# Latent attention and the start of a six-layer pipeline: keys and values from a folded weight, another split of small copies over two queues, and three pieces of work moved to other places

## The chip, the cores and the metric

The kernel runs on one core of one Trainium2 chip. A core has a matrix engine (PE, TensorE; PEld is its weight load), VectorE (DVE), ScalarE (ACT), GpSimd (POOL), and SyncE (SP), which here only issues DMAs. ScalarE and GpSimd can issue DMAs too. Each engine works through its own instruction list in order, and waits on semaphores for the others.

The metric is the device time of one execution in microseconds (us), lower is better. Times below are in us unless ns is said.

## The reference

Four residual blocks, each on the layer-normed stream, over 16 sequences of 256 tokens of 128 features, all in float32:

```python
x = x + latent_attention(layernorm(x), Wq, bq, Wl, bl, Wk, bk, Wv, bv, Wo, bo)   # 16 heads of 8
x = x + six_layers(layernorm(x), ...)    # 16 heads of 64, window 32, each with a gated MLP of 341
x = x + mamba(layernorm(x), ...)
x = x + two_layers(layernorm(x), ...)    # 8 heads of 64, window 64, each with a gated MLP of 341
```

The first of them is what most of the change touches:

```python
q = (x @ Wq + bq).reshape(B, S, H, Dh)
latent = x @ Wl + bl                       # 32 features
k = (latent @ Wk + bk).reshape(B, S, H, Dh)
v = (latent @ Wv + bv).reshape(B, S, H, Dh)
scores = jnp.einsum('bihd,bjhd->bhij', q, k) * SCALE
attn = jax.nn.softmax(scores, axis=-1)
out = jnp.einsum('bhij,bjhd->bihd', attn, v).reshape(B, S, D)
out = out @ Wo + bo
```

In a layer of the six, the output of attention is multiplied by a matrix Wo of 1024 rows, 64 per head; the value projection Wv has 64 columns per head.

## The kernel before

**Latent attention** (`latent_attention`). The 4096 tokens are cut into 8 tiles t of 512 tokens, that is two sequences. Three generators and four functions deal with a tile:

- `prepare(t)` transposes the tile, norms it (`normed`: a matmul with the centering matrix, squares on ScalarE, a matmul for the mean, rstd on GpSimd at L116, transposes of rstd at L167), makes the 32 latent features (L278, L280), and from them keys (L297) and values (L303); queries come from the normed x (L284). It has eight steps, divided by `yield`. All of them and `finish` use one PSUM bank (`bank`, pool la_m with one buffer).
- `spread`, within `prepare`, copies queries and keys, 16 small DMAs each (8 rows of 512), into padded tiles qa and ka, of which there are three of each. They go to SP and GpSimd in turn (L291).
- `maximum(m)` makes scores with PE (L328) and takes their row maxima with VectorE (L337); `subtract` writes the maxima, transposed, into a spare row of qa (L354, a DMA of ScalarE's queue); `weigh(m)` makes the transposed scores (L366) and exponentials (L376); `apply(m)`, for odd m only, multiplies with the values (L389) and copies the result to os (L398).
- `gather(t)` undoes the padding with 32 small DMAs, 16 to `sums` and 16 to `of` (L412): one row group in four on SP, the rest on GpSimd; of the last tile one half on each.
- `finish(t)` takes the reciprocal of the sums (L418), multiplies (L419), multiplies with Wo (px, L422), adds to x (L423), stores x to HBM (L424) and norms the result into the tile y, which the six layers read.

The loop at L432 runs m from -12 to 130, in an order written out by hand (`manual_schedule`): what is emitted first stands first on each engine. Tile t has the sixteen m from 16t on for `weigh`; `maximum` is 12 ahead. In each m there are the matmuls of `weigh(m)` and `maximum(m+12)` by turns, then either a `subtract` or one step of the generators in the list `steps`, then `apply(m-2)`. `prepare(t)` joins the list at m = 16(t-2), `finish(t)` at m = 16(t+1)+10, where its first step is emitted at once, ahead of the matmuls; `gather(t)` is emitted as a whole at m = 16(t+1)+1. What is emitted outside of such a stretch may be put earlier on an engine by the scheduler.

**The six layers** (`Pipeline` with PLAN32). A block is 128 tokens, 32 blocks a layer. In iteration i of `run`, the list PLAN32 names the steps and how many blocks each lags; block i is projected to q and k (L782) in iteration i. I call iteration i "block i" below. Norms of pairs of blocks come from a Newton iteration on GpSimd (`pair_newton`, L852 to L858), the output of a pair of blocks is multiplied with wvo, the product of Wv and Wo per head (L1086), five blocks later. wvo of a later layer is made two heads at a time beside `turn_y` in the blocks of the layer before (`coming`, `products`, `keep_y`). wvo of the first layer, and the offsets of its MLP (`offsets`, `add_offsets`), are made at i = 3, all at once, in `rest_of_ready` (L672). At i = 6 the `finish` of the last tile of latent attention, returned by it as `rest`, is run through at once. PSUM has four double banks here; the list after PLAN32 says which step uses which: pq, scores and the tiles pb and pm of `rest_of_ready` share one (o); yt, tk, tq, tp and u0 share another (s); `rest` uses q.

`load(0)` issues the first layer's weights on SP: wqkv in two halves, the scales sc, wo, wv, w1, w2. It comes after latent attention, since the weights take its place in memory. `tables` makes the rotation table from sc with VectorE (L690, L692).

Of the kernel before, what the change touches and what calls it, by code (L numbers as in the profile page):

```python
# [29 lines left out]
P = 128  # L30
# [158 lines left out]
def latent_attention(ctx: ExitStack, k: Stack, w, x_in, last, later):  # L189
# [9 lines left out]

    nc = k.nc
    H, D, LAT = 16, 8, 32
    SCALE = D**-0.5
# [7 lines left out]


    wq = wp.tile([P, P], F32, name="wq")
    wk = wp.tile([LAT, P], F32, name="wk")
    wl = wp.tile([P, LAT], F32, name="wl")
    wv = wp.tile([LAT, P], F32, name="wv")
    wo = last.tile([P, P], F32, name="wo")
    bq, bk, bo = (p.tile([P, 1], F32, name=n) for n, p in (("bq", wp), ("bk", wp), ("bo", last)))
    bl = wp.tile([LAT, 1], F32, name="bl")  # L220
    bv = wp.tile([P, P], F32, name="bv")
    for t, name in ((wl, "Wl"), (wq, "Wq"), (wk, "Wk"), (wv, "Wv"), (wo, "Wo")):
        nc.scalar.dma_start(t, w[name])
    for t, name in ((bl, "bl"), (bq, "bq"), (bk, "bk"), (bo, "bo")):
        nc.scalar.dma_start(t, w[name].unsqueeze(1))
# [32 lines left out]
    def prepare(t):  # L258

        ps = bank()  # L260
        xt = xs.pop(t)
        for j in range(4):
            nc.tensor.transpose(ps[:, j * P : (j + 1) * P], xt[:, j, :], k.ident)
        if 3 <= t + 2 < NTT:
            fetch(t + 2)
        pool = last if t == NTT - 1 else work
        x = xs[t] = pool.tile([P, TT], F32, tag="x", bufs=1 if t == NTT - 1 else 5, name=k.name("x"))
        nc.scalar.copy(x, ps)
        yield
        for step in k.normed(x, bank):  # L270
            if step is None:
                yield
        cen, ps = step
        xn = work.tile([P, TT], F32, tag="xn", bufs=1, name=k.name("xn"))
        nc.vector.tensor_mul(xn, cen, ps)
        yield
        ps = bank()
        nc.tensor.matmul(ps[0:LAT], wl, xn, start=True, stop=True)  # L278
        lat = work.tile([LAT, TT], F32, tag="lat", bufs=1, name=k.name("lat"))
        nc.scalar.activation(lat, ps[0:LAT], AF.Identity, bias=bl)  # L280
        yield
        q, kk = (work.tile([P, TT], F32, tag=i, bufs=1, name=k.name(i)) for i in "qk")
        ps = bank()
        nc.tensor.matmul(ps, wq, xn, start=True, stop=True)  # L284
        nc.vector.tensor_scalar(q, ps, bq, SCALE, ALU.add, ALU.mult)
        queues = (nc.sync, nc.gpsimd)

        def spread(src, dst):
            for r in range(4):
                for g in range(4):  # L290
                    queues[g % 2].dma_start(dst[32 * r : 32 * r + D, g], src[rows_of(r, g)])  # L291

        nc.sync.dma_start(qa[t % 3][D::32], row[:, 0:1].to_broadcast([4, 4, TT]))
        spread(q, qa[t % 3])
        yield
        ps = bank()
        nc.tensor.matmul(ps, wk, lat, start=True, stop=True)  # L297
        nc.scalar.activation(kk, ps, AF.Identity, bias=bk)
        spread(kk, ka[t % 3])
        yield  # L300
        ps = bank()
        for c in range(4):
            nc.tensor.matmul(ps[:, bass.ts(c, P)], lat[:, bass.ts(c, P)], wv, start=True, stop=True)  # L303
        nc.vector.tensor_add(
            va[t % 3][:, :, :, 0:D],
            ps.rearrange("p (c h d) -> p c h d", c=4, d=D),
            bv.rearrange("p (h d) -> p h d", d=D).unsqueeze(1).to_broadcast([P, 4, H, D]),
        )
        yield

    nms, oss, weights, outs = {}, {}, {}, {}

# [87 lines left out]
    def gather(t):  # L400

        os = oss.pop(t)
        o, sums = (
            (last if t == NTT - 1 else work).tile([P, TT], F32, tag=i, bufs=1, name=k.name(i))
            for i in ("of", "sums")
        )
        for dst, first in ((sums, D), (o, 0)):
            for r in range(4):
                rows = slice(32 * r + first, 32 * r + first + D)
                for g in range(4):  # L410
                    queue = nc.sync if g == 3 or (t == NTT - 1 and g == 2) else nc.gpsimd
                    queue.dma_start(dst[rows_of(r, g)], os[rows, g])  # L412
        outs[t] = o, sums

    def finish(t, bank):

# [8 lines left out]
        yield  # L425
        yield from k.norm_to_y(t, x, bank)

    for _ in prepare(0):
        pass
    AHEAD, steps = 12, []  # L430
    with k.tc.manual_schedule():
        for m in range(-AHEAD, 8 * B + 3):  # L432
            at = m + AHEAD
            if at == 0 or (at % 16 == 12 and at // 16 + 2 < NTT):
                steps.append(prepare(1 if at == 0 else at // 16 + 2))
            if at == 14:
                later()
            if m % 16 == 10 and m > 16:
                steps.append(finish(m // 16 - 1, bank))
                next(steps[-1])  # L440
            four = (
                weigh(m) if 0 <= m < 8 * B else (),
                maximum(at) if at < 8 * B else (),
            )
            for _ in zip_longest(*four):
                pass
            if at % 4 == 1 and 2 <= at <= 8 * B + 1:
                subtract(at - 2)
            else:
                while steps and next(steps[0], True):  # L450
                    steps.pop(0)
            if 2 <= m <= 8 * B + 1:
                apply(m - 2)
            if m % 16 == 1 and m > 16:
                gather(m // 16 - 1)
    return lambda bank: finish(NTT - 1, bank)


# [82 lines left out]
class Pipeline:  # L541
# [124 lines left out]

    def ready(self, l):

        self.tables(l)
        self.rest_of_ready(l)  # L670

    def rest_of_ready(self, l):  # L672
        k, nc, L = self.k, self.nc, self.layers[l]
        pb = k.wide(self.homes["scores"], "pb")[:, 0:6]
        self.offsets(l, pb)
        self.add_offsets(l, pb)
        if self.W == 64:
            return
        for c0 in (0, 4):
            pm = k.wide(self.homes["scores"], "pm").rearrange("p (i c d) -> p i c d", i=2, d=P)  # L680
            for c in range(4):
                self.products(l, c0 + c, pm[:, :, c])
            nc.scalar.copy(
                L.wvo[:, 2 * c0 : 2 * c0 + 8].rearrange("p (c i) d -> p i c d", i=2), pm
            )

    def tables(self, l):

# [40 lines left out]

    def coming(self, n):  # L730

        l, step = divmod(n, NBLK)
        return l + 1, step if l + 1 < self.depth else -1

    @staticmethod
    def beside(yt):

        return yt[:, P : P + 768].rearrange("p (i d) -> p i d", i=2)[:, :, 0:P]

    def run(self, rest=None):  # L740

        last = self.depth * NBLK
        self.work = self.work or self.pool("work", 2)
        if self.W == 64:
            self.ready(0)
        else:
            self.tables(0)
        with self.k.tc.manual_schedule():
            for i in range(last + max(lag for _, lag in self.plan)):
                if i % NBLK == 14 and i // NBLK + 1 < self.depth:  # L750
                    self.load(i // NBLK + 1)
                if i == 3 and self.W == 32:
                    self.rest_of_ready(0)
                if i == 6 and rest:
                    for _ in rest(lambda: self.k.wide(self.homes["norm"], "rest")[:, 0:TT]):
                        pass
                for (name, *args), lag in self.plan:
                    n = i - lag
                    if not 0 <= n < last:
                        continue  # L760
                    if name.startswith("ff_"):
                        if n % 4 == 0:
                            getattr(self, name)(n // 4, *args)
                    elif name.startswith("pair_"):
                        if n % 2 == 0:
                            getattr(self, name)(n, *args)
                    else:
                        getattr(self, name)(n, *args)
# [140 lines left out]
    def turn_y(self, n):  # L909

        L, b, blk = self.at(n)
        t0 = self.W + blk * P
        yt = self.bank(n, "yt")
        self.nc.tensor.transpose(yt[:, 0:P], self.k.y[:, b, t0 : t0 + P], self.k.ident)
        l, step = self.coming(n)
        if step == 17:
            self.tables(l)
        if 18 <= step < 26:
            self.products(l, step - 18, self.beside(yt))
        if step == 26:  # L920
            self.offsets(l, yt[:, P : P + 6])

    def keep_y(self, n):
# [2 lines left out]
        l, step = self.coming(n)  # L926
        if 18 <= step < 26:
            c = 2 * (step - 18)
            self.nc.scalar.copy(self.layers[l].wvo[:, c : c + 2], self.beside(yt))
        if step == 26:  # L930
            self.add_offsets(l, yt[:, P : P + 6])

    def spread(self, n):
# [614 lines left out]
def tile_kernel(ctx: ExitStack, tc: tile.TileContext, a, out):  # L1548
# [8 lines left out]
    with ExitStack() as stack:  # L1557
# [2 lines left out]
        rest = latent_attention(k, every("L0_attn_"), a["L0_attn_x"], last, pipe.setup)  # L1560
        with k.pairs():
            pipe.open()
            pipe.run(rest)
    with ExitStack() as stack:
        pipe = Pipeline(k, stack, part("L1_ffn_"), 8, 64, a["rope64"], 2, PLAN64, out)
        pipe.setup()
# [31 lines left out]
```

## Time and profile before

| | us |
|---|---|
| median of 3 runs (lowest to highest) | 4891.48 (4888.69 to 4897.18) |
| profiled execution, its own time | 4885.07 |
| its span, first to last instruction | 4883.2 |
| mean granted TensorE clock (1 is full) | 0.974 |
| latent attention, first scores to last `apply` | 34 to 420 |
| first load of wqkv issued | 420.5 |
| filling of the six-layer pipeline | 420 to about 600 |

Busy time of the engines within the stretch from 290 to 335 us, one period of latent attention, and the idle time before the operation and what ended it:

| operation | engine | count | mean ns | idle before |
|---|---|---|---|---|
| L328, scores | PE | 136 | 401 | 1.5, for the reductions L337 |
| L366, transposed scores | PE | 136 | 402 | 0.1 |
| L389, values | PE | 128 | 385 | 0 |
| L167, transposes of rstd | PE | 8 | 285 | 2.6, for GpSimd L116 |
| L337, maxima | DVE | 33 | 688 | 13.9, for L328 |
| L418, reciprocal | DVE | 1 | 3345 | 0 |
| L376, exponentials | ACT | 33 | 595 | 10.0 |
| L412, gathers to sums | POOL | 12 | 523 | 1.4 |
| L291, spreads of keys | POOL | 8 | 519 | 0 |

A float32 matmul appears as two records, so the counts of PE are twice those in the code; four matmuls with 32 rows run beside one another, so their records overlap. The issue of a DMA is busy time on GpSimd, but not on SP or ScalarE. A wait is counted for the engine that stands still, and named after what came last.

### The profile page before, as it was taken

Reading aid. Unit: us, or ns where it says so; the run is one execution under the profiler, and the core shown is the slowest. Engines: PE = TensorE matmul, PEld = TensorE weight load, DVE = VectorE, ACT = ScalarE, POOL = GpSimd, SP = SyncE. Lnnn points to the kernel's source line nnn. Section 1 sums busy time; section 2 is a strip of 40 time slices with the busy share of each in tenths; the row PEclk is TensorE's granted clock in tenths of the full one; section 3 lists DMA queues with packets and bytes.
Section 4 is the critical chain, followed back from the end, with each engine's and each line's share of the span. In section 5 each row is a group of like instructions: output and inputs, shape, how many; then the busy total and the mean of one; then the engine's idle time right before and its main releaser. Section 6 shows DMA issues by size and latency. Waiting matters only on the chain.

```text
span 4883.2 us, 121363 instructions
## 1 busy us (share of the span) xinstructions
PE 4587.9 (94%) x50842; PEld 3063.1 (63%) x50842; DVE 3372.6 (69%) x4048; ACT 2743.4 (56%) x3417; POOL 3317.8 (68%) x3643
## 2 busy tenths in 40 slices
PE   8896799999999999999999999999996998899998
PEld 4453566666666666666666666666664665566665
DVE  4663677777777777777777777777772765788774
ACT  3553466566656666566666566665663453565654
POOL 3444677777777777777777777787783454777774
PEclk9997899999999999999999999999998898999999
DMA  1111010000100010001000010000101000111111
GB/s 35 37 29 43 14 39 17 16 16 18 39 16 16 17 39 16 16 17 39 16 16 16 17 39 16 17 17 22 26 23 41 15 12 18 53 47 43 49 56 39
DMA packets 208778, 131.54 MB, mean 27 GB/s; under 512 B 62029, under 2 KB 180153, under 8 KB 208233
## 3 DMA queue, kind: packets, MB, share of 16 engines
q1 hardware_dynamic: 196456, 118.12, 9.7%
q0 software_dynamic: 9984, 5.14, 0.6%
q8 instruction: 403, 6.60, 0.6%
q14 instruction: 143, 1.16, 0.1%
q10 hardware_dynamic: 1792, 0.51, 0.1%
HBM read 29.65 MB, written 8.39 MB: 8 GB/s over the span
## 4 chain that ended last, share of the span: by engine, by line
PE 69%; DVE 14%; POOL 7%; issue 5%; ACT 4%; SPq 0%; DMA 0%; DVEq 0%; ACTq 0%; POOLq 0%
PE py L1086 13%; PE pq L782 7%; PE hid L1143 6%; PE u L1060 6%; PE scores L973 5%; PE pk L782 5%; PE tq L872 4%; PE tp L1019 3%; DVE n L839 3%; PE fy L1177 3%; PE tk L872 2%; DVE rotq L807 2%; POOL rstd L116 1%; PE scores L955 1%; DVE t2q L819 1%
## 5 line engine op out<-in xcount | busy, mean ns | idle before, releaser
L1086 PE MATMUL py<-oT,wvo 128*128 128x256 f32 x3072 | 679.1, 379 | 1.2 <-ACT oT L1073 1.2
L1013 POOL TENSOR_TENSOR pr<-pr,rs 128x1024 f32<-128x1024 f32 x256 | 489.8, 1913 | 273.5 <-DVE rs L1008 241.4
L843 POOL TENSOR_TENSOR rotq<-rotq,t2q 128x1024 f32<-128x1024 f32 x256 | 605.0, 2363 | 37.0 <-DMA w<-in_L_ffn_W 22.2
L1086 PEld LDWEIGHTS py<-oT,wvo 128*128 128x128 f32 x3072 | 577.1, 190 | 75.1 <-ACT oT L1073 1.6
L1073 ACT COPY oT<-u 128x1024 f32<-128x1024 f32 x384 | 377.5, 1014 | 316.3 <-PE u L1060 307.6
L782 PE MATMUL pq<-wqkv,y 128*128 128x512 f32 x1024 | 495.6, 607 | 15.3 <-DVE t2q L819 5.4
L863 POOL TENSOR_TENSOR rotq<-rotq,rn 128x1024 f32<-128x1024 f32 x256 | 488.8, 1909 | 11.2
L807 DVE TENSOR_TENSOR rotq<-pq,tab 128x1024 f32<-128x1024 f32 x256 | 313.4, 1224 | 235.9 <-ACT sqq L793 150.5
L101 DVE TENSOR_TENSOR y<-y,py 64x256 f32<-64x256 f32 x256 | 107.2, 419 | 524.7 <-PE py L1086 523.0
L889 ACT COPY qT<-tq 128x1024 f32<-128x1024 f32 (+1 forms) x256 | 230.7, 901 | 410.9 <-PE tq L872 410.9
L843 POOL TENSOR_TENSOR rotk<-rotk,t2k 128x1024 f32<-128x1024 f32 x192 | 454.0, 2364 | 0.0
L1004 DVE TENSOR_REDUCE rs<-pr 128x16 f32<-128x1024 f32 (+1 forms) x256 | 312.3, 1220 | 157.7 <-ACT pr L997 152.9
L973 PEld LDWEIGHTS scores<-kT,qT 64*32 64x32 f32 (+1 forms) x26624 | 320.7, 108 | 157.9 <-issue 97.2
L793 ACT ACTIVATE sqq<-pq 128x1024 f32<-128x1024 f32 x256 | 261.8, 1023 | 263.1 <-PE pq L782 250.7
L1060 PE MATMUL u<-prT,vc 64*128 64x256 f32 x3072 | 405.5, 395 | 1.9
L973 PE MATMUL scores<-kT,qT 64*32 64x64 f32 (+2 forms) x26624 | 398.8, 225 | 3.0 <-issue 1.4
L782 PE MATMUL pk<-wqkv,y 128*128 128x512 f32 x768 | 393.3, 602 | 6.8 <-DMA wqkv<-in_L_ffn_Wqkv 6.8
L1143 PE MATMUL hid<-fxn,w 128*128 128x512 f32 (+1 forms) x768 | 388.9, 618 | 5.4 <-DVE ga L1165 2.7
L852 POOL TENSOR_SCALAR rn<-n 128x64 int32<-128x64 int32 (+1 forms) x128 | 30.3, 236 | 530.6 <-DVE n L839 530.6
L863 POOL TENSOR_TENSOR rotk<-rotk,rn 128x1024 f32<-128x1024 f32 x192 | 365.4, 1903 | 0.1
L997 ACT ACTIVATE pr<-pr 128x1024 f32<-128x1024 f32 x256 | 270.6, 1057 | 135.9 <-DVE pr L989 122.2
L984 DVE TENSOR_REDUCE nm<-scores 128x16 f32<-128x1024 f32 (+1 forms) x256 | 312.1, 1219 | 22.0 <-PE scores L973 20.6
(265 smaller groups left out, 9835.2 us busy)
## 6 DMA issues: line engine op xcount, KB each, us to landing
vc<-vt SPq DMA_DIRECT2D x1152, 32.0 KB
vc<-vt SPq DMA_DIRECT2D x64, 256.0 KB
vc<-vt SPq DMA_DIRECT2D x96, 128.0 KB
vc<-vt SPq DMA_DIRECT2D x576, 16.0 KB
xd<-x SPq DMA_DIRECT2D x24, 256.0 KB
wqkv<-in_L_ffn_Wqkv SPq DMA_DIRECT2D x12, 512.0 KB
x<-xd SPq DMA_DIRECT2D x24, 256.0 KB
wo<-in_L_ffn_Wo SPq DMA_DIRECT2D x6, 512.0 KB
```

The lines of the kernel that those rows point to most:

```text
L782: self.nc.tensor.matmul(pq[:, 512 * int(half) : 512 * int(half) + 512], self.k.y[:, b, c0 : c0 + P], L.wqkv[:, col : col + 512], start=Tru ...
L807: self.nc.vector.tensor_mul(rot.rearrange("p (w h) e -> p w h e", w=ways), self.get(n, "p" + group).rearrange("p (w h e) -> p w h e", w=wa ...
L843: self.nc.gpsimd.tensor_add(rot, rot, self.done(n, "t2" + group))
L863: self.nc.gpsimd.tensor_mul(rot, rot, rn.unsqueeze(2).to_broadcast(list(rot.shape)))
L973: self.nc.tensor.matmul(sc[ch * W : (ch + 1) * W, par, c, first : self.KS], qT[rows, c, ch * W : (ch + 1) * W], kT[rows, c, t0 - W + first ...
L984: self.nc.vector.tensor_reduce(nm, self.get(n, "scores"), AX.X, ALU.max, negate=True)
L1004: self.nc.vector.tensor_reduce(rs, self.by_head(n), AX.X, ALU.add)
L1013: self.nc.gpsimd.tensor_mul(pr, pr, rs)
L1060: self.nc.tensor.matmul(pu[:, par, :, j, :], self.vc[n % 3][rows, ch, :], prT[rows, :, ch * W : (ch + 1) * W], start=True, stop=True,)
L1073: self.nc.scalar.copy(self.get(n - blk, "oT")[:, :, q0 : q0 + 64].rearrange("p (c i) q -> p i c q", i=2), self.done(n, "u" + half).rearran ...
L1086: self.nc.tensor.matmul(py, w[:, c, :], oT[:, c, :], start=(c == 0), stop=(c == last))
L1143: self.nc.tensor.matmul(pg[0:n, at : at + TT], L.w1[:, col : col + n], self.get(t, "fxn"), start=True, stop=True,)
```

## The change

- The host gives the transposed Wl as well (WlT). A new function `fold`, called after the second step of `prepare(0)`, multiplies Wl with Wk and with Wv, and bl with them for the biases. Keys and values come straight from the normed x with these 128x128 weights; the step with the latent features is gone, so `prepare` has seven steps.
- Spreads go to SP alone from tile 2 on; tiles 0 and 1 keep the turns of SP and GpSimd.
- Gathers go to GpSimd alone, but for the last tile, half of which stays on SP. `gather` is a generator of eight steps with four DMAs each, one step in each m from 16(t+1)+1 on. What is left of it after the loop is emitted behind the loop, outside of the order written out by hand.
- `finish(t)` joins at m = 16(t+1)+11, one later, and behind the step of that m.
- First layer: `rest_of_ready` is gone. `products` come beside `turn_y` in blocks 1 to 4, four heads each, and the offsets in block 6; `keep_y` copies them.
- The `finish` of the last tile is run one step a block from block 3 on.

```diff
+    wk0, wv0, wlT = (wp.tile([LAT, P], F32, name=n) for n in ("wk0", "wv0", "wlT"))
+    wk, wv = (wp.tile([P, P], F32, name=n) for n in ("wk", "wv"))
...
-        ps = bank()
-        nc.tensor.matmul(ps[0:LAT], wl, xn, start=True, stop=True)
-        lat = work.tile([LAT, TT], F32, tag="lat", bufs=1, name=k.name("lat"))
-        nc.scalar.activation(lat, ps[0:LAT], AF.Identity, bias=bl)
-        yield
...
-        queues = (nc.sync, nc.gpsimd)
+        queues = (nc.sync, nc.gpsimd if t < 2 else nc.sync)
...
-        nc.tensor.matmul(ps, wk, lat, start=True, stop=True)
+        nc.tensor.matmul(ps, wk, xn, start=True, stop=True)
...
-            nc.tensor.matmul(ps[:, bass.ts(c, P)], lat[:, bass.ts(c, P)], wv, start=True, stop=True)
+            nc.tensor.matmul(ps[:, bass.ts(c, P)], xn[:, bass.ts(c, P)], wv, start=True, stop=True)
...
+    def fold():
+        for dst, of, bias, lhsT, rhs in (
+            (wk, wk0, None, None, None),
+            (wv, wv0, None, None, None),
+            (bk, None, bk, wk0, bl),
+            (bv, None, bv, bl.to_broadcast([LAT, P]), wv0),
+        ):
+            ps = bank()[:, 0 : dst.shape[1]]
+            if of is not None:
+                nc.tensor.matmul(ps, wlT, of, start=True, stop=True)
+                nc.scalar.copy(dst, ps)
+            else:
+                nc.tensor.matmul(ps, lhsT, rhs, start=True, stop=True)
+                nc.vector.tensor_add(dst, bias, ps)
...
-                    queue = nc.sync if g == 3 or (t == NTT - 1 and g == 2) else nc.gpsimd
+                    queue = nc.sync if t == NTT - 1 and g > 1 else nc.gpsimd
                     queue.dma_start(dst[rows_of(r, g)], os[rows, g])
+                yield
...
-    for _ in prepare(0):
-        pass
+    for i, _ in enumerate(prepare(0)):
+        if i == 1:
+            fold()
...
-            if m % 16 == 10 and m > 16:
-                steps.append(finish(m // 16 - 1, bank))
-                next(steps[-1])
...
+            if m % 16 == 11 and m > 16:
+                steps.append(finish(m // 16 - 1, bank))
+                next(steps[-1])
             if 2 <= m <= 8 * B + 1:
                 apply(m - 2)
             if m % 16 == 1 and m > 16:
-                gather(m // 16 - 1)
+                pieces = gather(m // 16 - 1)
+            next(pieces, None)
+    for _ in pieces:
+        pass
...
     def coming(self, n):
         l, step = divmod(n, NBLK)
+        if self.W == 32 and n < 8:
+            return 0, n + 40
...
-                if i == 3 and self.W == 32:
-                    self.rest_of_ready(0)
-                if i == 6 and rest:
-                    for _ in rest(lambda: self.k.wide(self.homes["norm"], "rest")[:, 0:TT]):
-                        pass
+                if i >= 3:
+                    next(rest, None)
...
-        if step == 26:
+        if 41 <= step < 45:
+            for c in range(2):
+                self.products(
+                    l, 2 * (step - 41) + c, self.beside(yt)[:, :, P * c : P * c + P]
+                )
+        if step in (26, 46):
             self.offsets(l, yt[:, P : P + 6])
...
+        if 41 <= step < 45:
+            c = 4 * (step - 41)
+            self.nc.scalar.copy(
+                self.layers[l].wvo[:, c : c + 4].rearrange("p (c i) d -> p i c d", i=2),
+                self.beside(yt)[:, :, 0 : 2 * P].rearrange("p i (c d) -> p i c d", d=P),
+            )
```

## The prediction

> **What bounds the kernel now.** I read the page first, then the stretches of 20 us, then TensorE's waits, then the chain of waits and the timeline where those pointed.
>
> The page's head and four stretches (columns: busy us and count of PE, PEld, DVE, ACT and POOL, then granted clock, DMA share, GB/s):
>
> ```profile
> span 4883.2 us, 121363 instructions
> ...
> PE 4587.9 (94%) x50842; PEld 3063.1 (63%) x50842; DVE 3372.6 (69%) x4048; ACT 2743.4 (56%) x3417; POOL 3317.8 (68%) x3643
> ...
> 300.00:320.00 20.00, 17.86 (x210) 9.85 (x212) 11.02 (x18) 12.32 (x25) 11.20 (x22) 1.00 0.16 28
> ...
> 420.00:440.00 20.00, 8.17 (x17) 2.46 (x9) 0.23 (x1) 2.68 (x4) 2.11 (x5) 0.58 0.36 95
> ...
> 480.00:500.00 20.00, 14.66 (x194) 10.09 (x193) 8.96 (x12) 6.80 (x8) 2.05 (x2) 0.71 0.01 2
> ...
> 540.00:560.00 20.00, 10.80 (x32) 6.10 (x31) 9.08 (x10) 2.09 (x3) 8.06 (x5) 0.66 0.04 14
> ```
>
> PE leads the whole span. The diff touches only latent attention (0 to 420 us), where PE is about 89% busy, and the filling of the first pipeline (420 to 600 us), where PE idles and its clock falls. Behind 600 us the two programs are the same, so what these 600 us gain or lose is the result. TensorE's waits from 60 to 420 us (total, times, longest):
>
> ```profile
> PE m L167 <- POOL rstd L116: 14.7, 11, 3.3
> PE s L328 <- DVE nm L337: 8.4, 6, 1.6
> PE st L366 <- ACT pT L376: 5.0, 13, 0.7
> PE m L422 <- issue: 2.8, 1, 2.8
> ```
>
> The first is rstd on GpSimd queued behind 24 gathers; the second and fourth are VectorE's reciprocal. The timeline shows both, and two short stretches what a gap does to the clock:
>
> ```profile
> 311.16 0.65 PE L167 MATMUL m<-ident,rstd 128*128 128x128 f32 x4 [2.05 <-POOL rstd L116]
> ...
> 363.60 3.35 DVE L418 RECIPROCAL sums<-sums 128x512 f32<-128x512 f32 x1
> ...
> 367.78 1.10 PE L422 MATMUL m<-of,wo 128*128 128x512 f32 x2 [2.80 <-issue]
> ...
> 214.00:216.00 2.00, 0.00 (x0) 0.00 (x0) 0.52 (x1) 0.23 (x1) 1.98 (x4) 0.78 0.37 56
> 216.00:218.00 2.00, 1.61 (x8) 1.24 (x12) 0.38 (x1) 0.00 (x0) 0.34 (x1) 0.50 0.01 3
> ```
>
> In the fill, the chain (start, us, what) names two pieces that the change takes away:
>
> ```profile
> 474.70 4.04 issue
> 478.74 2.43 PE pb L702 x12
> ...
> 487.89 3.79 PE pq L782 x4
> ...
> 541.83 1.22 DVE rs L1004
> 543.05 3.27 DVE sums L418
> ...
> 558.14 2.66 PE pq L782 x4
> ```
>
> From 478.74 to 487.89 everything waits for block 3's offsets and products of Wv and Wo; from 541.83 to 558.14 for the last tile's finish.
>
> **The change, part by part** (us; minus is gain). A slot is one m of the attention loop, on average 2.75 (44 per tile of 16).
>
> *Latent step gone.* The matmul at L278 costs 1.04 warm at 315.42 and 1.85 cold at 51.29: six tiles by 1.04 and tile 1 by 1.85, -8.1. It lies on PE, back to back, so it counts in full; ScalarE's lat (0.68) is off the path. K over 128 rows instead of 32 (644 against 588 ns a pass, L149 against L297): +0.8 over seven tiles.
>
> *Start.* Tile 0 loses L278 to L284, 18.19 to 20.87: -2.7. fold() puts four matmuls through the one bank between center and mean: 0.52 each for two (a quarter of L303's 2.07), 0.47 each for two (a quarter of L157's 1.87), and four evacuations of 0.27 (L925) with some 0.06 of handing over: 3.3. Bounds 2.0 (evacuations hidden) and 5 (a late weight). Net +0.6.
>
> *Queues.* POOL loses 96 spreads and gains 56 gathers, at 0.52 each. GpSimd doesn't wait for PE between gathers, so the eight steps only decide what stands ahead of rstd: 12 gathers from slot 1 (6.2) instead of 24, and rstd is due at slot 4 (8.3 later). The finish step now straddles the tile boundary, so prepare begins at slot 2, and its transposes come at slot 6, two slots behind rstd. The five waits of 2.05, 2.06 and 3.26 go: -11.5. The finish's own waits of 0.56 (four) go too, since an apply now lies between; against them, q at slot 7 comes one slot behind xn and waits about 0.45 for the multiply at L275, five times: 0 together. SP takes all 32 spreads of a tile, at 0.68 each (5.43 for 8 at 23.76): 22 instead of 11, from slot 7, with the next fetch and xd behind them, for which nobody hurries. They are due at slot 20, 33 later after q's evacuation and 2.2 of landing. SP's dearest row of small copies, 1.0 each (3.03 for 3 at 567.50), makes 32. Price 0; if the cover went, each late us counts on six tiles.
>
> *A new wait.* finish is appended at slot 11, behind that slot's reductions, and px stands at slot 12; in between PE has only apply(9) (1.0) and one group of scores (1.1). v ends four reductions and one add before it, so on VectorE the reciprocal starts some 1.4 after PE has ended slot 11's scores, and needs 4.05 with the multiply: px waits 1.4+4.05+0.1-2.1 = 3.45. The row at 367.78 is the same order with less before it, 2.80. Queued behind px are all scores; ScalarE's exponentials wait for those. Before, the reciprocal cost 1.5 on five tiles (7.6 of the 8.4) and 2.8 on the sixth; now 6 times 3.45 = 20.7: +10.3. Tile 6 has no reductions left ahead of it: 0. Bounds: -10.4 (all hidden) to +16 (a whole 4.05+0.4 each).
>
> *Clock.* After the gaps at 214, 235, 264 and 365 the clock stood at 0.50 for about 6.8, 6.8, 3.4 and 3.4: half of 20.4 lost, 10.2. Gaps of 2.8 or more closed it in both cases, 2.05 in one of four, 1.5 in one of five. I take five closings of the six new gaps at 5.0 each: 12.5 lost, so +2.3 (bounds -10.2 with none, +10.2 with six long ones).
>
> The Trainium skill ("TensorE: Matmul & The Clock Gate", Part 1: The HAM clock gate) has the gate close after an idle window of about 3.4 us and reopen after about 3.4 us of work, in free-running windows. The cold stretches agree in length (3.4 and twice that); the closing after a 1.5 us gap at 234.9 doesn't. By the rule alone all six new waits would close it for one window, 10.2 lost: this term would be 0 and the sum 2.3 lower. It speaks against the change all the same: gaps of 2.05 become gaps of 3.45.
>
> Attention together: -8.1+0.8+0.6-11.5+10.3+2.3 = -5.6.
>
> *Fill, its start.* The first half of wqkv stood among SP's last gathers (issued 420.50); now both halves come behind all sixteen. Another 512 KB at the 204 to 255 GB/s of 422 to 434 is 2.0 to 2.6, ahead of the scale rows that released the first rotation (441.83); one more gather precedes the last copy, -0.6. +2 (bounds 0 and +4, a whole transfer with its latency).
>
> *Block 3.* project(3) can start at 478.74: -9.15. But the reciprocal and multiply of the last tile now stand on VectorE behind total (ends 480.98), and end near 485.6, where cosine would start at 483.7: +2.0.
>
> *Block 4.* px ahead of project, cold: 2.1. Products: 4 matmuls a block, a quarter of 2.08 times two, 1.05 on PE ahead of the second half of K; in blocks 1, 2 and 3 it hides, because rotk waits for VectorE 1.6 longer (pk ready 493.53, rotk 495.16); in block 4 scores wait for kT: +1.0. Together +3.1. The copies of wvo (four of 512 columns instead of two of 1024 at 1.01) lie on ScalarE, idle 3.9 before 491.76; the two VectorE steps on w1 and b1 (0.8) go to block 6: 0.
>
> *Blocks 5 to 7.* center +1.1 in block 5. Block 6 loses 541.83 to 558.14, -16.3, and 0.9 of cold clock (2.66 against 1.73 for project); it gains mean 1.1 and offsets 1.3. Block 7: transposes +0.65. If none of the added PE work is hidden by the newton on GpSimd, that is all of it.
>
> Fill: +2-9.15+2+3.1+1.1-16.3-0.9+2.4+0.65 = -15.1. Bounds: -24 (additions hidden) and -6 (half of the two gaps refills with the newton's wait, 13.5 at 463.09).
>
> **Sum:** -20.7. The profiled run took 4885.07 (span 4883.2 and 1.9 around it), 6.4 below the median of the runs shown. 4885.07-20.7 = 4864.4; on the median's level 4891.48-20.7 = 4870.8.
>
> **Rivals.**
> 1. *The new wait is no longer than the old.* If px finds `of` as the reciprocal's other waiters do now (1.5, once 2.8), +10.3 becomes 0, and with two closings (5 lost instead of 10.2) +2.3 becomes -5.2: -38.5, 4853. For it: in the last tile VectorE is early. Against: 367.78.
> 2. *The fill is bound elsewhere.* If blocks 3 and 6 wait for GpSimd's newton anyway, the fill gives -5 and the whole -11, 4881. For it: tq waits 22.5 in total for POOL there. Against: both gaps stand ahead of project, and the newton starts only behind it.
> 3. *Slower: the spreads come late.* One queue with 32 copies: it decides from 1.03 us a copy (33 over 32). At 1.2 they end 5.6 late on six tiles, +34, so +13: 4905. For it: 1.0 was seen. Against: 0.68 on the same copies.
> That the change doesn't do what it says is possible for the eight steps alone (GpSimd runs ahead of them), and the sum counts it so.
>
> **How the numbers follow.** Forecast 0.53 (-12 to -29: 4862 to 4880), rival 1 0.17, rival 2 0.20, rival 3 0.10. The time is the forecast's, 4871. The range takes rival 1's middle and rival 2 down to -4: 4853 to 4887. About 0.2% (9.8 us) is what a measurement of this kernel can tell from no change. Faster: 0.53, 0.17 and a fifth of rival 2, 0.74; same 0.16; slower 0.10.
>
> **What would show it.** Right: no L167 wait of 2 us; a wait of 3 to 3.6 at px on VectorE, six times, most with 0.50 behind it; project(3) some 7 earlier after block 2; block 6 without the gap of 16; wqkv behind the gathers. Wrong: scores waiting for a DMA of qa or ka (rival 3), no wait at px (rival 1), or blocks 3 and 6 as long as before though the chain shows no rest and no products (rival 2).

## The result, and the profile after

The changed kernel takes 4879.8 us (median of 18 runs, 4872.3 to 4887.9), the kernel before 4890.1 in its 18 runs beside it: ratio 0.998, 95% interval 0.9972 to 0.9988. It is 10 us faster, where the prediction's sum said 20.7. The first block below is the head of the profiled execution of the changed kernel. The second has four stretches with the columns of those shown of before: busy us and count of PE, PEld, DVE, ACT and POOL, granted clock, DMA share, GB/s.

```profile
span 4881.5 us, 121165 instructions
...
PE 4588.6 (94%) x50834; PEld 3063.9 (63%) x50834; DVE 3375.5 (69%) x4058; ACT 2738.2 (56%) x3405; POOL 3297.5 (68%) x3603
```

```profile
420.00:440.00 20.00, 8.89 (x78) 4.48 (x76) 1.54 (x3) 4.96 (x11) 6.34 (x12) 0.70 0.16 37
480.00:500.00 20.00, 14.68 (x219) 8.38 (x219) 18.03 (x16) 8.34 (x11) 10.05 (x5) 0.83 0.06 13
540.00:560.00 20.00, 18.11 (x175) 13.58 (x181) 12.37 (x16) 7.42 (x8) 18.93 (x21) 1.00 0.05 10
300.00:320.00 20.00, 18.86 (x220) 11.55 (x223) 11.73 (x20) 13.31 (x27) 9.69 (x17) 1.00 0.13 31
```

The gap at 540 to 560 is gone: PE is busy 18.11 there, not 10.80. Where the time went is read from two milestones that both kernels have: the first and the last copy of os on ScalarE (the first and last apply), and the start of the square of q of block 9 (sqq from pq), behind which the two programs are the same. The first two columns of this table are start times in each run's profile; the two stages are differences of these and of the start of block 9's square. The last column is how long the clock stood at half, from 60 us to the last apply, added up from the record of the granted clock; half of it is lost.

| kernel | first apply | last apply | first to last | last apply to block 9 | half clock |
|---|---|---|---|---|---|
| before | 86.97 | 420.50 | 333.5 | 184.3 | 24 |
| changed | 89.36 | 429.65 | 340.3 | 167.8 | 31 |
| fill only | 86.98 | 425.93 | 339.0 | 166.4 | 34 |
| attention only | 90.02 | 431.62 | 341.6 | 183.4 | 41 |
| finish at 10 | 89.78 | 424.78 | 335.0 | 168.1 | 44 |
| nmT on GpSimd | 97.86 | 435.81 | 338.0 | 164.8 | 48 |
| finish at 12 | 87.13 | 419.93 | 332.8 | 165.5 | 31 |
| nmT later | 89.35 | 425.08 | 335.7 | 165.7 | 34 |
| both | 90.07 | 419.95 | 329.9 | 165.9 | 27 |
| spread split | 89.35 | 443.32 | 354.0 | 164.8 | 58 |
| latent kept | 86.98 | 433.94 | 347.0 | 164.5 | 34 |
| gather once | 89.34 | 477.07 | 387.7 | 166.5 | 85 |
| split reciprocal | 89.89 | 406.36 | 316.5 | 165.9 | 17 |
| fold in gap | 88.22 | 403.77 | 315.6 | 165.7 | 14 |

The fill gave 16.5 (184.3 to 167.8). Attention, which was to give 5.6, lost 9.2 at the last apply. The spans of the two profiles differ by 1.7 only, since the stretch from block 9 to the end, where the programs are the same, took 4278.4 in the profile of before and 4284.1 in this one; in the fourteen profiles of the table it takes 4270.4 to 4286.9. So one profile says which stage changed, and only the medians say by how much the whole did. TensorE's waits in the changed kernel's attention (60 to 430 us; total, times, longest) say with what. L435 is px, L379 and L341 are the two kinds of scores (L366 and L328 before), L364 the transposes of the maxima (L351 before):

```profile
PE m L435 <- DVE of L432: 20.0, 6, 3.4
PE st L379 <- ACT pT L389: 11.4, 15, 2.4
PE m L364 <- DVE y L180: 5.1, 6, 0.9
PE s L341 <- DVE nm L350: 2.1, 3, 0.8
...
PE m L167 <- POOL rstd L116: 0.2, 1, 0.2
```

rstd's 14.7 are gone and px's 20.0 have come, both as predicted. Two rows were not: st waits 11.4 for pT (5.0 before), and the transposes wait 5.1 for y, a wait that didn't exist. The first is explained by the timeline around one of the long ones, all engines (start, us, engine, line, what, in brackets the idle time before and what ended it):

```profile
97.16 11.41 SPq L288 DMA_DIRECT2D qa<-q  x16
...
103.54 0.56 ACT L366 COPY nmT<-m 4x512 f32<-4x512 f32 x1
...
106.45 0.56 ACTq L367 DMA_DIRECT2D qa<-nmT  x1
107.06 0.37 ACT L411 COPY os<-o 128x256 f32<-128x256 f32 x1 [2.96 <-DMA qa<-q]
107.33 1.09 ACT L389 ACTIVATE pT<-st 128x512 f32<-128x512 f32 x2
...
107.98 0.48 PE L379 MATMUL st<-qa,ka 32*128 32x256 f32 x1 [2.40 <-ACT pT L389]
```

The sixteen copies of q now stand in one row on SP. ScalarE has nmT ready at 104.1, but issues its write only at 106.45, and what released it is a DMA of SP's copies. In the trace, SP's and ScalarE's DMAs take eight semaphores in turn, and a DMA waits until the last one that used its semaphore has landed. The one due to the write had gone to a copy that SP issued at 104.35 and that landed at 106.38. So ScalarE stood still, two exponentials were late behind it, and TensorE waited 2.40. The same happens with nmT of 113.8, 144.6 and 205.4 (2.4, 2.1, 2.3 late), and shorter at 252.3 and 297.4 (1.1, 1.3). The kernel before has this wait too: behind its rows of eight copies, six of the 32 writes are 0.9 to 1.0 late, each released by the landing of a copy of q.

In the fill, the chain of waits of the changed kernel (start, us, what) has these pieces:

```profile
439.47 3.81 DMA wqkv<-in_L_ffn_Wqkv
...
489.96 3.75 PE pq L786 x4
...
512.68 1.71 PE rest L435 x2
...
540.24 6.91 PE py L1101 x32
...
548.81 1.84 PE pq L786 x4
```

There is no issue gap of 4.04 and no products ahead of block 3's project (489.96), and project of block 6 comes at 548.81, behind py, the transposes tq and one step of the finish, without a gap.

### The profile page after: what moved, and what is told of

Same layout as the page of the kernel before. It is cut to its first block, busy times and chain, and to the rows that moved or that the text cites. A ratio compares the mean times of both kernels' runs of the same rounds, so it can differ in the third digit from the quotient of the medians.

```text
span 4881.5 us, 121165 instructions
## 1 busy us (share of the span) xinstructions
PE 4588.6 (94%) x50834; PEld 3063.9 (63%) x50834; DVE 3375.5 (69%) x4058; ACT 2738.2 (56%) x3405; POOL 3297.5 (68%) x3603
## 3 DMA queue, kind: packets, MB, share of 16 engines
q14 instruction: 140, 1.15, 0.1%
## 4 chain that ended last, share of the span: by engine, by line
PE 70%; DVE 15%; POOL 6%; ACT 4%; issue 3%; SPq 1%; DMA 0%; DVEq 0%; ACTq 0%; POOLq 0%
PE py L1101 13%; PE pq L786 7%; PE hid L1158 6%; PE u L1075 6%; PE scores L988 5%; PE pk L786 5%; PE tq L876 4%; PE tp L1034 3%; DVE n L843 3%; PE fy L1192 3%; PE tk L876 2%; DVE rotq L811 2%; PE st L379 2%; DVE rotk L811 1%; PE scores L970 1%
## 5 line engine op out<-in xcount | busy, mean ns | idle before, releaser
L847 POOL TENSOR_TENSOR rotq<-rotq,t2q 128x1024 f32<-128x1024 f32 x256 | 605.0, 2363 | 38.3 <-DMA vc<-vt 36.6
L116 POOL TENSOR_TENSOR rstd<-var,neg_half 128x4 f32<-128x4 f32 (+1 forms) x112 | 110.9, 990 | 339.1 <-DVE var L161 228.1
```

The source lines that it names most:

```text
L847: self.nc.gpsimd.tensor_add(rot, rot, self.done(n, "t2" + group))
```

## Experiments

All are compared with runs of the kernel before on the same chip (medians 4891.1 to 4892.7). Where a difference from the changed kernel has two numbers, one is by the medians and one by the ratios to before.

**Fill alone, attention alone.** The first kernel is before's latent_attention with the changed Pipeline, the second the reverse.

> The kernel before with the change's fill alone (products and offsets of the first layer in blocks 1 to 6, the last tile's finish one step a block). Theory: the fill's gain stands by itself, as the two profiles show it from the last apply to block 9 (184.3 us before, 167.8 after: -16.5), and attention stays as it was, so the time is 4872 to 4876, some -16 against before and below the changed kernel by 5 to 8. Rival: part of the fill's gain comes from attention's new order (gathers in eight steps, wqkv behind them), then fill alone gives -8 or less, 4882 and more.

> The changed kernel with its fill undone: attention alone is changed. Theory: the profiles' +9.2 at the last apply is real and not the luck of one execution, so the time is 4895 to 4900, +5 to +9 against before; TensorE waits of 60 to 420 us about 40 in sum, px 20. Rival (attention as predicted, -5.6, and the loss seen in one profile chance): 4883 to 4886.

Fill alone: 4874.5, ratio 0.9958 (0.9945 to 0.997), -17 by the medians and below the changed kernel: the fill's gain stands by itself. Attention alone: 4896.7, ratio 1.0007 (0.9998 to 1.0016): +5 by the medians, +3 by the ratio, so not the -5.6 of the prediction, nor the whole +9.2 of the pair of profiles. Its waits are 38.3, px's 20.0 among them, as expected. The table says why: the fill-only kernel has before's attention, instruction for instruction, and needs 339.0 from first to last apply where before's profile shows 333.5. The clock stood at half for 34 us in it, not 24; half of that difference is 5.1 of the 5.4, and TensorE's waits are nearly the same. The profile of before was a lucky one; its own time, 4885.07, is 5 below the median. Against the other, the changed attention loses 1.3 from first to last apply and 2.4 ahead of it, 3.7 in all.

**Where the finish stands.** Slot 10 ahead of the matmuls, as before, and slot 12.

```diff
-            if m % 16 == 11 and m > 16:
+            if m % 16 == 12 and m > 16:
```

> The changed kernel with the finish step joined at slot 10 ahead of the slot's matmuls, as before. Theory: the px wait of 20 us on six tiles is the price of the slot; it goes back to reductions waiting for the reciprocal (some 8) and the clock closes in fewer gaps, so -12 in waits and -2 to -6 in clock: 14 to 18 below the changed kernel, 4862 to 4866. Rival: ScalarE is late at that place anyway, so another wait takes the place of px's: within 4 of the changed kernel.

> The changed kernel with the finish step joined one slot later (12), so that its px stands at slot 14 with a whole slot of scores, the transposed maxima and an apply ahead of it. Theory: px's waits (20.0 on six tiles) go, reductions of slot 13 wait for the reciprocal 1.5 on five tiles (7 to 8) and the clock closes in fewer gaps (27 us of half clock in the changed kernel's attention, perhaps half of it): 14 to 19 below the changed kernel, 4861 to 4866. Rival: steps one slot later are too late, the copies of q and k (sixteen in a row on SyncE) then hold up the scores of the next tile, and a wait on their DMA comes in: same or slower, 4880 and more.

Slot 10: 4871.8, ratio 0.9958 (0.9946 to 0.9971), 8 to 11 below the changed kernel, not 14 to 18. Its waits of TensorE:

```profile
PE m L435 <- ACT pT L389: 14.4, 5, 2.9
PE st L379 <- ACT pT L389: 7.4, 14, 2.2
PE m L435 <- issue: 2.8, 1, 2.8
...
PE m L435 <- DVE of L432: 1.8, 1, 1.8
```

px still waits 19.0, now on all seven tiles of the loop. (The first row puts it down to pT; in the first of them, the multiply ended at 150.15 and px began at 150.26.) My theory was wrong about what before did: there the tile's latent step kept prepare busy through slot 10, so px came a slot later, 5.9 behind the reciprocal's start. With the latent step gone, prepare has no step left at slot 10 and px follows in the same slot. What this kernel saves is the wait for y (5.1), 4 of st's and 1 of px's.

Slot 12: 4869.9, ratio 0.996 (0.9947 to 0.9974), some 10 below the changed kernel:

```profile
PE s L341 <- DVE nm L350: 13.3, 9, 2.0
PE st L379 <- ACT pT L389: 11.7, 21, 2.3
PE m L265 <- DVE y L180: 3.4, 4, 0.9
PE m L167 <- POOL rstd L116: 2.7, 5, 0.6
```

px no longer waits at all, since the whole of slot 13 and the scores of slot 14 lie between the reciprocal and it. But scores now wait 13.3 for the reductions behind the reciprocal, more than the 7 to 8 expected: about half of px's wait changes its name. No scores wait for a DMA of qa or ka, so the later steps are not too late.

**The write of the maxima.** First on GpSimd for all tiles, then from the second tile on (the edit below; the columns of qa are left out in it):

```diff
-        nc.scalar.dma_start(qa[t % 3][D::32, ...], nmT)
+        (nc.gpsimd if t else nc.scalar).dma_start(qa[t % 3][D::32, ...], nmT)
```

> The changed kernel with the write of the transposed maxima issued by GpSimd in place of ScalarE. Theory: on ScalarE this write waits for a semaphore that it shares with SyncE's copies of q and k (sixteen in a row now, 0.68 each), and holds back the exponentials behind it, 1.1 to 2.4 us in each of some six places; off ScalarE these waits go: TensorE's wait of st for pT falls from 11.4 to about 5 and the time is 5 to 8 below the changed kernel, 4872 to 4875. Rival A: the exponentials are late for another reason, the wait stays near 11 and the time within 2. Rival B: the write comes late behind the gathers on GpSimd and st waits for it by DMA, 1 to 2 us in each of six tiles: 6 to 12 above.

> As the run with the maxima's write on GpSimd, but the first tile's four writes stay on ScalarE. Theory: that run lost 8.5 ahead of the first apply (one wait of 6.7 for the maxima, GpSimd still busy with copies of q and k) and won 6.7 behind it; with the start left alone only the gain is left: last apply 5 to 7 earlier than in the changed kernel, time 4873 to 4876. Rival: what was won behind the first apply was the start's delay being taken up (slack that came back), then nothing is left: within 2 of the changed kernel.

On all tiles: 4881.3, ratio 0.9975 (0.9965 to 0.9985), no gain, and neither theory nor rivals had the reason. From first to last apply it is 2.3 shorter, but the first apply is 8.5 late. In the timeline, GpSimd's third write waits for ScalarE's copy until 83.5, and behind it stands later()'s set-up of masks, which now runs into 88. VectorE's sixteen casts of pick (L503) wait for that, the reductions stand behind the casts, and one group of scores waits 6.73 for its maxima:

```profile
92.07 0.79 PE L341 MATMUL s<-ka,qa 32*128 32x256 f32 x1 [6.73 <-DVE nm L350]
```

From the second tile on only: 4873.9, ratio 0.9965 (0.9952 to 0.9977), 6 to 7 below the changed kernel, with intervals that overlap a little, and the waits are those of the theory:

```profile
PE m L435 <- DVE of L432: 20.0, 6, 3.4
PE st L379 <- ACT pT L389: 5.9, 14, 0.7
```

st's wait is back to 5.9 with none over 0.7; px is untouched. With the landing above this shows the semaphore mechanism and its price against this profile: 5.5 of waits. The price varies: attention alone, with the same attention program as the changed kernel, has 8.9 for st in its profile, not 11.4, which makes it 3.0 there.

**Both edits in one.**

> Both edits in one kernel. Theory: the px wait and the write's wait are two mechanisms and add up: 20 to 26 below the changed kernel, 4854 to 4860. Rival: one hides the other (ScalarE catches up in the px gap): no better than the better one of the two by more than 2.

4868.2, ratio 0.9954 (0.9942 to 0.9967): the rival's time, no better than slot 12 alone by more than 2. What is left is mostly the wait for the reductions behind the reciprocal:

```profile
PE s L341 <- DVE nm L350: 13.9, 9, 2.0
```

Compared with slot 12 alone, st's wait falls from 11.7 to 7.9 and first to last apply by 2.9, but the first apply is 2.9 later, where the two programs differ in nothing; so in these profiles a gain of about 3 met a loss by chance of about 3. That the edits add up at least in part is likely, and not shown by the times.

**Copies split between SP and GpSimd, as before.**

```diff
-        queues = (nc.sync, nc.gpsimd if t < 2 else nc.sync)
+        queues = (nc.sync, nc.gpsimd)
```

> The changed kernel with the copies of q and k split between SyncE and GpSimd for all tiles, as before. Theory: with eight copies in a row in place of sixteen the semaphore that ScalarE's write shares is free in time, st's wait for pT goes from 11.4 to 5 or 6; GpSimd takes 16 copies a tile more (8.3 us), in slots where rstd isn't due: 4 to 7 below the changed kernel, 4873 to 4876. Rival: rstd or the gathers come behind them on GpSimd and rstd's wait comes back (some 10 us on five tiles): 4884 to 4890.

4886.4, ratio 0.9985 (0.9977 to 0.9994), 2 to 7 above the changed kernel, with intervals that overlap; in the profile the last apply is 13.7 later. Half of the additional half clock (58 against 31 us) is as much as that; the waits are only some 3 more. The waits, then GpSimd's timeline in one tile:

```profile
PE m L435 <- DVE of L432: 28.2, 6, 7.0
PE st L379 <- ACT pT L389: 7.0, 13, 2.0
```

```profile
139.12 4.10 POOL L288 DMA_DIRECT2D qa<-q  x8 [1.50 <-DVE q L282]
143.22 2.06 POOL L425 DMA_DIRECT2D of<-os  x4
145.26 4.10 POOL L288 DMA_DIRECT2D ka<-k  x8
149.36 4.10 POOL L425 DMA_DIRECT2D of<-os  x8
```

st's wait fell, as the semaphore theory has it. But the last eight gathers now stand behind sixteen copies and end at 153.5, the multiply waits for them, and px waits up to 7.0. So the split gains nothing beside gathers in eight steps: it trades ScalarE's late write for a late multiply.

**The latent step kept; the gathers in one piece.** The first restores the matmul by Wl and the path through lat, without fold(); in the second the only yield stands behind all 32 gathers.

> The changed kernel with the latent step kept (matmul by Wl, lat, then keys and values from it over 32 rows) and without the folding at the start; queues, gathers, finish and fill as changed. Theory: the step costs TensorE what the prediction took for it, 8.1 less 0.8 for keys over 128 rows, less 1.6 that the first scores came later in the changed kernel: 5 to 7 above the changed kernel, 4885 to 4887. Rival: the steps of each tile end two slots earlier without it only to meet other waits, so TensorE loses the same time elsewhere: within 2.

> The changed kernel with all 32 gathers of a tile issued at slot 1 in one piece, still on GpSimd. Theory: 32 by 0.52 is 16.6 us of GpSimd, rstd is computed behind them some 3 us behind slot 6, where its transposes stand (13.7 behind slot 1): TensorE waits for rstd 3 to 5 us on six tiles, and the clock closes in these gaps: 20 to 35 above the changed kernel, 4900 to 4915. Rival: steps in eight pieces are not needed, rstd now stands two slots further back: within 4.

Latent kept: 4884.0, ratio 0.9989 (0.9979 to 0.9999), some 4 above the changed kernel, with intervals that overlap. First to last apply is 6.7 longer, 1.7 of it clock; that leaves 5.0, with waits that are nearly the same in sum. For the six tiles that have their latent step in that stretch the prediction's terms give 6 x (1.04-0.11) = 5.6. But the first apply is at 86.98, as before, and not at 89.36: the folding costs 2.4 there. The nine profiles whose program is the changed one up to there have it at 87.1 to 90.1, eight of them at 89.3 or later, so the 2.4 is typical and not one execution's chance. One piece: 4926.8, ratio 1.0075 (1.0062 to 1.0088), 47 above, over the 20 to 35 expected:

```profile
PE m L167 <- POOL rstd L116: 34.9, 6, 10.5
```

The waits for rstd are 35, and the half clock grows from 31 to 85, another 27. So the eight steps do matter, and by what the prediction names: they decide what stands ahead of rstd.

**A version that beats both kernels.** The write on GpSimd from the second tile on, and the division in three slots, 10, 11 and 12; in the second kernel also fold() one step later.

```diff
-        nc.vector.reciprocal(sums, sums)
+        for cols in (slice(0, TT),) if t == NTT - 1 else (slice(0, TT // 2), slice(TT // 2, TT)):
+            nc.vector.reciprocal(sums[:, cols], sums[:, cols])
+            if t < NTT - 1:
+                yield
...
-            if m % 16 == 11 and m > 16:
-                steps.append(finish(m // 16 - 1, bank))
-                next(steps[-1])
+            if m % 16 in (10, 11, 12) and m > 16:
+                if m % 16 == 10:
+                    divide = finish(m // 16 - 1, bank)
+                next(divide)
+                if m % 16 == 12:
+                    steps.append(divide)
```

```diff
-        if i == 1:
+        if i == 2:
             fold()
```

> The changed kernel with the maxima's write on GpSimd from the second tile on, and the reciprocal cut into two halves of 256 columns at slots 10 and 11, the multiply at slot 12, px at slot 14. Theory: with px at slot 14 what was left was reductions behind a reciprocal of 3.35 (13.9 of waits for the maxima); halves of 1.7 fit beside a slot's reductions, these waits fall to 3 to 6, and the time is 4 to 10 below the kernel with both edits: 4857 to 4864. Rival: VectorE is late by the sum, not by the piece (4.05 on a tile either way): waits stay above 10 and the time 4866 to 4872.

> The kernel with the split reciprocal, and the folding moved one step back, from between center and mean to between mean and the transposes of rstd, where TensorE waits 1.4 for the newton on GpSimd. Theory: the folding holds up the first tile by its whole 4.3 where it stands, and by 4.3 less 1.4 there: first scores at 34.5 to 34.8 in place of 35.85, first apply 1 to 1.5 earlier, and the time within 3 of the kernel with the split reciprocal (4855 to 4861), since 1.2 is under what these runs can tell. Rival: the first tile's copies to the 32-row groups start on their queues' own time, then the first scores don't move (35.7 to 35.9).

Split reciprocal: 4857.3, ratio 0.9936 (0.9924 to 0.9948). VectorE in one tile, and TensorE's waits:

```profile
145.37 1.74 DVE L432 RECIPROCAL sums<-sums 128x256 f32<-128x256 f32 x1
147.03 1.22 DVE L350 TENSOR_REDUCE nm<-s 128x2 f32<-128x512 f32 x2
148.17 1.74 DVE L432 RECIPROCAL sums<-sums 128x256 f32<-128x256 f32 x1
149.83 1.22 DVE L350 TENSOR_REDUCE nm<-s 128x2 f32<-128x512 f32 x2
150.96 0.68 DVE L435 TENSOR_TENSOR of<-of,sums 128x512 f32<-128x512 f32 x1
```

```profile
PE st L379 <- ACT pT L389: 7.9, 19, 0.7
PE s L341 <- DVE nm L350: 5.2, 10, 0.9
PE m L167 <- POOL rstd L116: 3.8, 5, 0.9
PE m L265 <- DVE y L180: 3.4, 4, 0.9
```

The halves fit between reductions; the wait for the maxima falls from the 13.9 of the kernel with both edits to 5.2, and no wait is longer than 0.9. The time is 9 to 11 below that kernel's. Attention waits 20 in all, half of the changed kernel's 40.7, and the clock stood at half for 17 us, not 31: 20 and 7 less, together about the 24 that first to last apply is shorter.

Fold in the gap: 4851.2, ratio 0.9913 (0.9899 to 0.9927), the best of all. TensorE at its start:

```profile
12.91 1.87 PE L157 MATMUL m<-mean_w,sqn 128*128 128x1 f32 x8 [1.16 <-ACT cen L153]
15.03 0.79 PE L318 MATMUL m<-wk,wlT 32*128 32x128 f32 x2 [0.25 <-DVE var L161]
16.18 0.79 PE L318 MATMUL m<-wv,wlT 32*128 32x128 f32 x2 [0.35 <-ACT wk L319]
17.32 0.58 PE L321 MATMUL m<-bl,wk 32*128 32x1 f32 x2 [0.35 <-ACT wv L319]
18.16 0.79 PE L321 MATMUL m<-wv,bl 32*128 32x128 f32 x2 [0.25 <-DVE bk L322]
19.42 1.09 PE L167 MATMUL m<-ident,rstd 128*128 128x128 f32 x4 [0.47 <-DVE bv L322]
```

The transposes come at 19.42, not 20.50, and the first scores at 34.77, not 35.92: 1.15 earlier, as the theory said. Block 9 is 2.8 earlier. The time fell by 6 by the medians and 11 by the ratios, which these 2.8 don't explain; behind block 9 the programs are the same, and so the rest is put down to chance.

## Why the prediction was off by half

- **The fill: right.** -15.1 predicted, -16.5 in the profiles, -17 alone. By stage, from one block's sqq to the next: block 3 -8.5 (predicted -7.15), block 4 +2.9 (+3.1), block 5 +1.3 (+1.1), blocks 6 and 7 together -13.6 (-14.15). The start is +1.4 up to block 2 (+2).
- **The new wait at px: right**, 20.0 for 20.7, six times up to 3.4. TensorE's waits for the maxima went from 8.4 to 2.1, for rstd from 14.7 to 0.2 (-14.5 for -11.5). The 3.0 more are mostly the finish's own waits of 0.56, of which there were five and not four; the new wait at q that the prediction set against them came to 0.8.
- **Queues: the step that failed.** "Price 0" looked only at whether the 32 copies land in time, and they do. It left out who else uses what they use. ScalarE's write of the maxima takes its turn at the same eight semaphores, and behind a row of sixteen copies it waits up to 2.4. That is +6.4 in st's waits, 5.5 of which the run with the write moved takes back. Rival 3 named the same queue, but not this way.
- **The finish across the tile boundary: a wait overlooked.** The prediction saw that prepare then begins at slot 2, and counted only the gain for rstd. The maxima's transposes at slot 1 now come straight behind y's multiplies and want their bank: six times 0.9, +5.1. Finishing at slot 10 has none of it; at slot 12 it becomes the 3.4 of L265.
- **Start: mis-sized.** fold() takes 4.3 (12.92 to 17.21), not 3.3: its matmuls are 0.58 to 0.79 in the cold clock, and TensorE is idle 0.25 to 0.38 behind each. So the first scores come 1.6 later, not 0.6 (34.28 to 35.85). The first apply comes 2.4 later, so the 1.85 of tile 1's latent matmul isn't gained ahead of it; why not stays open. Together -1.25 was predicted there and +2.4 came.
- **Latent step: right** in the loop (5.0 for 5.6), see above.
- **Clock: within chance.** +2.3 predicted. Half of 31-24 is +3.4, and each of px's six waits has a stretch of half clock at it, five of 3.4 and one of 6.8; but two profiles of before's own attention differ by 5.

Waits were to change by -1.2 (-11.5+10.3) and changed by +9.3 (31.4 to 40.7). That 10.5, the 3.6 at the start and 1.1 of clock turn -5.6 into +9.6; attention did +9.2 in the pair of profiles, and some +4 when the luck of before's profile is left out. The measured time lies near rival 2's 4881, but that is a coincidence and not by rival 2's reason: the fill gave everything, attention gave it back. Rival 1 fell with px's wait.

## What to carry to other kernels

When DMAs move to another queue, ask not only whether they land in time but what they share with the DMAs of other engines: here an engine that issues one small write stood still because a semaphore that it was due had gone to the long row. A step on an in-order engine that is longer than the slack beside it is cheaper in pieces: two halves of a reciprocal in two slots took away most of the waits that moving the whole of it had left under another name. And a stage's profile should be taken from more than one execution before its difference is believed, where the clock alone moves it by 5 us, as here.

## What the runs showed of the hardware

The record of the granted clock shows stretches of half clock of 3.4 us and its multiples. In the changed kernel those of the attention loop begin at 154.77, 202.55, 212.79, 250.34, 294.71, 339.09 and 380.05: apart by 14, 3, 11, 13, 13 and 12 times 3.413. The Trainium skill ("TensorE: Matmul & The Clock Gate", Part 1: The HAM clock gate) has a free-running window of 3413 ns, and this agrees. It also has the gate close after an idle window of about 3.4 us, and here the runs differ. In the kernel with the split reciprocal no wait in the loop is over 0.9, and the clock still closes four times in it between 230 and 400. One of these, by stretches of 2 us (columns as above):

```profile
230.00:232.00 2.00, 2.00 (x33) 1.35 (x26) 2.00 (x4) 0.37 (x1) 0.00 (x0) 1.00 0.13 25
232.00:234.00 2.00, 1.38 (x10) 0.57 (x12) 2.00 (x3) 1.08 (x2) 0.00 (x0) 1.00 0.14 29
234.00:236.00 2.00, 2.00 (x22) 1.06 (x22) 2.00 (x4) 1.47 (x3) 0.00 (x0) 0.83 0.16 33
236.00:238.00 2.00, 2.00 (x20) 0.95 (x16) 0.06 (x1) 0.43 (x2) 0.60 (x1) 0.50 0.16 28
```

TensorE was idle for 0.62 in all of 230 to 234, and still the clock fell to 0.50. It may be that whether a gap closes it depends on where the gap falls on the grid, which would explain why the same program's attention took 333.5 once and 339.0 another time; this isn't shown, and what the gate counts as busy was not tried.
